# GpSimd takes the differences of the next input, and four v tiles are made later, in a two-layer attention kernel

## The chip, the cores and the metric

The kernel runs on one core of a Trainium2 chip. The metric is the device time in microseconds (us), the median of several runs. Engines are named as in the profile: PE is TensorE (PEld its weight loads), DVE is VectorE, ACT is ScalarE, POOL is GpSimd, and SP is SyncE, which here only issues DMAs.

## The reference, cut to what matters

Two attention layers run on `x` of shape (8, 512, 32, 32): 8 batches, 512 channels, 1024 positions, all float32. Layer 1, the only one that the change touches, is

```
y    = group_norm(x)                                # input of layer 1
q, k, v = w_q y, w_k y, w_v y                       # 512x512 products, 8 heads of 64
attn = softmax(w_head mixed over heads(q k^T * scale))
attn = (attn - mean) / sqrt(var + eps) * gamma + beta   # over a whole head
x    = x + w_proj (attn v) + b_proj
```

The mix over heads needs the scores of all 8 heads for the same query and key, before the exponential.

## The kernel before, in words

Layer 0 runs first, for all batches (up to about 1790 us of the profile). Layer 1 then runs batch by batch, each taking some 273 us. What follows is about layer 1.

**Order.** Nothing schedules at run time: each engine carries out its own instructions in the order in which the Python code issues them, waiting on semaphores where it depends on another engine or on a DMA. SP has one such queue for nearly all DMAs. An `Agenda` holds small jobs by slot number; `ag.at(slot, fn)` enters one, and `Attention1.step` (L1857) calls `ag.run` with fixed slots: 4p-0.5 and 4p-0.25 around the first mix of step p, 4p+0.5 and 4p+1.5 in its middle, and 4p+t at the end of quarter t.

**Steps.** A batch has nine steps, p = 0 to 8, each of four quarters t = 0 to 3. Step p makes eight score tiles for block p of the queries (`scores`, L1630), unless p = 8, and finishes the mix of block p-1 and the weighted values of blocks p-1 and p-2.

- `scores` writes a PSUM tile of 128x1024. There are three such tiles (tag `m`), taken in turn by scores, mixes, projections and v tiles. A copy (ACT L1642; in the first step every second one DVE L1640) takes it to SBUF as `raw`. Scores 0 to 3 fill one `raw` buffer and 4 to 7 the other; there are two.
- `regroup` (L1648) moves `raw` to `re` by 16 DMAs of 256 KB a step, 8 for each half, all in SP's queue. A half's buffer is free for the next step's copies when its 8 DMAs have landed.
- `mix` (L1667) multiplies `re` with the head weights into two of the PSUM tiles, and ACT takes the exponential `e` (L1680). DVE transposes it (`flip`, `et`, L1695, two buffers) and takes its statistics (`moments`, `bn`, L1709).
- `values` (L1725) multiplies `et` with `v`. Three times a batch (after blocks 1, 3 and 5) POOL's queue sends reciprocals to DRAM and reads them back spread over the partitions in two halves (`zd`, `rzb`, L1773 and L1783), and POOL multiplies a quarter of the output by them (`divide`, L1810).

**v tiles.** A batch has eight tiles of `v`. `v_pair(b, i)` makes tiles 2i and 2i+1 with four products each (L1456), and ACT and DVE copy them out of PSUM (L1462). Pairs 0 and 1 are made before the batch starts, pairs 2 and 3 (`NV` and `NV + 1`) inside it. `v_pair` reads the input `y_t[b]` and the weights `wv`, and `wv` lies in one of the two `et` buffers.

**The next input.** In steps 1 to 4, at the end of quarter 0, `piece` issues one transfer of 512 KB each of the next batch's input: `y_piece` (L1339), in SP's queue. The tile that it fills has the tag `n`, in a pool with one buffer: it is the buffer of this batch's `y`. In the last batch the pieces are weights instead (`p_piece`, L1333), with a buffer of their own.

**The ninth step.** In step 8 no scores are left, and the first four of the seven products of the next batch's k projection stand between the mixes (`k_go`, PE L1381). Some read `right_t`, four differences of blocks of the next `y`, each of 128x1024, made by `combine_right` (L1356); products 6, 7, 5 and 4 read the second, third, first and fourth difference. The buffer of `right_t` is one of the two of `raw`. Each product has a follower on ACT or DVE, such as `u = u + product` (L1396, L1398).

Of the kernel before, what the change touches and what calls it, by code (L numbers as in the profile page):

```python
# [467 lines left out]
def tile_two_attention_layers(  # L468
# [19 lines left out]
    nc = tc.nc  # L488
# [4 lines left out]
    NT = T // P  # L493
# [172 lines left out]
    def group_stages(b0, b1, psum):  # L666

        gs = GroupStats(
            gstat, psum, mvs[:, b0:b1].rearrange("p b c s -> p (b c) s"), f"1_{b0}", keep=1
        )  # L670

        def end():
            gs.root()
            at = slice(b0 * NCC, b1 * NCC)
            nc.vector.tensor_copy(gmean[:, at], gs.gm)
            nc.vector.tensor_copy(grstd[:, at], gs.r1)
            nc.vector.scalar_tensor_tensor(
                gneg[:, at], gs.gm, -1.0, gs.r1, ALU.mult, ALU.mult
            )
            nc.vector.scalar_tensor_tensor(  # L680
                ys[:, b0:b1].rearrange("p b c -> p (b c)"), gs.dm, float(T), gs.r1,
                ALU.mult, ALU.mult,
            )

        return gs.means, gs.squares, end
# [13 lines left out]
    with ExitStack() as l0:  # L699
# [177 lines left out]
        def combine_right(nm, n):  # L877

            if not tmp:
                for i in range(7):  # L880
                    tmp[i] = epool.tile([P, 2, FB], F32, tag="e", name=f"tmp_{nm}_{i}")
            b11, b12, b21, b22 = (n[:, 2 * i : 2 * i + 2, ts(j, FB)] for i in (0, 1) for j in (0, 1))
            nc.vector.tensor_sub(tmp[0], b12, b11)
            nc.vector.tensor_sub(tmp[1], b22, tmp[0])
            nc.vector.tensor_sub(tmp[2], b22, b12)
            nc.vector.tensor_sub(tmp[3], b21, tmp[1])
# [318 lines left out]
        for b in range(B):  # L1205
            more = b + 1 < B
            ag = Agenda()
# [61 lines left out]
    with ExitStack() as l1:  # L1269
# [15 lines left out]
        def m_psum(nm):  # L1285
            return ps_m.tile([P, 2, FB], F32, tag="m", name=nm)
# [4 lines left out]
        y_t, qo_t, k_t, v_t = ({0: t["1"]} for t in (n_t, q_t, k_t, v_t))  # L1291
# [12 lines left out]
        def left_piece(key, f, n):  # L1304

            if f == 0:
                left_tile(key)
            nc.sync.dma_start(
                out=w_t[key][:, f : f + n].rearrange("p f o -> p (f o)"),
                in_=left_d[key[0] + "1"][:, 2 * f * HC : 2 * (f + n) * HC],  # L1310
            )
# [23 lines left out]
        def y_piece(b, c):  # L1335

            if c == 0:
                y_t[b] = shared.tile([P, NCC, T], F32, tag="n", name=f"y_{b}")
            nc.sync.dma_start(out=y_t[b][:, c], in_=x1_d[b][ts(c, P), :])  # L1339

        def normalize1(b, c):
            normalize_to(y_t[b][:, c], b, c)
# [5 lines left out]
        def quarters(n):  # L1348
            return [[n[:, 2 * i : 2 * i + 2, ts(j, FB)] for j in range(2)] for i in range(2)]

        def combine_right(t, n, parts=range(4)):

            (b11, b12), (b21, b22) = quarters(n)
            for i in parts:
                x, y = ((b12, b11), (b22, t[:, 0]), (b22, b12), (b21, t[:, 1]))[i]
                nc.vector.tensor_sub(t[:, i], x, y)  # L1356

        class Projection:
            ORDER = (1, 6, 2, 7, 5, 3, 4)
# [55 lines left out]
        right_t = {}  # L1415

        def right_tile(b):

            right_t[b] = rawpool.tile([P, 4, 2, FB], F32, tag="raw", name=f"right_{b}")

        def left_p(b):

            t = rawpool.tile([P, H * FB], F32, tag="raw", name=f"left_p_{b}")
            load_left(("p", b), t[:, : 14 * HC])

        def right_y(b, parts=range(4)):
            combine_right(right_t[b], y_t[b], parts)

        def k_projection(b):
            t = k_t[b] = shared.tile([P, NCC, T], F32, tag="k", name=f"k1_{b}")  # L1430

            def finish(i, j, x, y):
                dst = t[:, 2 * i : 2 * i + 2, ts(j, FB)]
                if y is None:
                    nc.scalar.copy(dst, x)
                else:
                    nc.vector.tensor_add(dst, x, y)

            return Projection(f"pk1_{b}", ("k", b), y_t[b], right_t[b], finish)
# [3 lines left out]
        def k_leave():  # L1443
            for fn in due:
                fn()
            due.clear()

        def v_pair(b, i, ms=range(2)):

            if i == 0:  # L1450
                v_t[b] = shared.tile([P, NT, C], F32, tag="v", name=f"v1_{b}")
            ps = m_psum(f"pv1_{b}_{i}_{ms[0]}")
            w = w_t["v", b]
            for m in ms:
                for c in range(NCC):
                    nc.tensor.matmul(  # L1456
                        ps[:, m], y_t[b][:, c, ts(2 * i + m, P)], w[:, c],
                        start=(c == 0), stop=(c == NCC - 1),
                    )
            for m in ms:  # L1460
                copy = nc.vector.tensor_copy if m else nc.scalar.copy
                copy(v_t[b][:, 2 * i + m], ps[:, m])  # L1462
# [478 lines left out]
        NV = NT // 4  # L1941
        for b in range(B):
            more = b + 1 < B
            a = Attention1(b)
            ag = Agenda()
            ag.at(1, lambda: v_pair(b, NV))
            ag.at(3, lambda: v_pair(b, NV + 1, [0]))
            ag.at(3.75, lambda: v_pair(b, NV + 1, [1]))
            if b == 0:
                stages = group_stages(B - 1, B, small_psum1)  # L1950
                for i in range(3):
                    ag.at(i, stages[i])
                ag.at(3, v_sums)
            if more:
                a.pieces += [lambda c=c: y_piece(b + 1, c) for c in range(NCC)]
                a.pieces += [lambda f=f: left_piece(("k", b + 1), f, 2) for f in (0, 4)]
                ag.at(4 * NT, lambda: left_piece(("k", b + 1), 2, 2))
                ag.at(4 * NT, lambda: left_piece(("k", b + 1), 6, 1))
                for c in range(NCC):
                    ag.at(20 + c, lambda c=c: normalize1(b + 1, c))  # L1960

                def k_go(*ms):
                    if not kp:
                        kp.append(k_projection(b + 1))
                    for m in ms:
                        kp[0].products(m)
                        due.append(lambda m=m: kp[0].leave(m))

                kp = []
                ag.at(4 * NT - 0.5, lambda: right_tile(b + 1))  # L1970
                ag.at(4 * NT - 0.5, lambda: k_go(1))
                ag.at(4 * NT, lambda: right_y(b + 1, [0, 1]))
                ag.at(4 * NT + 0.5, lambda: k_go(2))
                ag.at(4 * NT + 1, lambda: right_y(b + 1, [2, 3]))
                ag.at(4 * NT + 1, lambda: left_p(b))
                ag.at(4 * NT + 1.5, lambda: k_go(6))
                ag.at(4 * NT + 2.5, lambda: k_go(7))
            else:
                a.pieces += [lambda c=c: p_piece(c) for c in range(NCC)]
            for p in range(NT + 1):  # L1980
                for t in range(4):
                    a.step(p, t, ag)
            ag.flush()
            k_leave()
            last = NT - 1
            a.sums(NCH - 1)
            if not more:
                a.values(last, 0, 2, 3)
                a.leave(last, 0)
                a.values(last, 1, 0, 1, 2, 3)  # L1990
                a.leave(last, 1)
                a.totals(NCH - 1)
                a.broadcast(1)
                a.instance()
                out1_last(a)
                continue
            k_go(5)
            a.values(last, 0, 2, 3)
            a.leave(last, 0)
            load_wv(b + 1)  # L2000
            a.values(last, 1, 0, 1, 2, 3)
            a.leave(last, 1)
            a.totals(NCH - 1)
            a.broadcast(1)
            a.instance()
            k_leave()
            k_go(4, 3)
            k_leave()
            a.instance_end()
            v_pair(b + 1, 0)  # L2010
            a.divide(NCH - 1)
            for g in range(H):
                a.affine(g)
            right_o = re_t[:, 4:8]
            combine_right(right_o, out_view(b))
            op = out1(b, right_o)
            load_left(("q", b + 1))
            v_pair(b + 1, 1)
            a.check()
            op.run()  # L2020
            q_projection(b + 1).run()
# [70 lines left out]
```

## Time and profile before

| | us |
|---|---|
| median of 3 runs | 3967.3 (3964.85 to 3968.17) |
| the profiled execution, its own time | 3964.89 |
| its span, from first to last instruction | 3963.1 |
| PE busy | 3874.9 (98% of the span) |
| DVE busy | 2769.6 (70%) |
| ACT busy | 1971.4 (50%) |
| POOL busy | 141.2 (4%) |
| mean granted clock of PE | 0.996 |

The times of single instructions come from the profiled execution. A row of the timeline gives the start in the span, the duration, engine, line, operation, the tile written and those read, the shape, and in brackets how long the engine stood idle just before and what ended that. Rows of SP (marked SPq) are the issue of a DMA, not its transfer. A matmul's end is modelled, so a PE that is busy is not always a PE at its peak.

### The profile page before, as it was taken

Reading aid. Unit: us, or ns where it says so; the run is one execution under the profiler, and the core shown is the slowest. Engines: PE = TensorE matmul, PEld = TensorE weight load, DVE = VectorE, ACT = ScalarE, POOL = GpSimd, SP = SyncE. Lnnn points to the kernel's source line nnn. Section 1 sums busy time; section 2 is a strip of 40 time slices with the busy share of each in tenths; the row PEclk is TensorE's granted clock in tenths of the full one; section 3 lists DMA queues with packets and bytes.
Section 4 is the critical chain, followed back from the end, with each engine's and each line's share of the span. In section 5 each row is a group of like instructions: output and inputs, shape, how many; then the busy total and the mean of one; then the engine's idle time right before and its main releaser. Section 6 shows DMA issues by size and latency. Waiting matters only on the chain.

```text
span 3963.1 us, 95453 instructions
## 1 busy us (share of the span) xinstructions
PE 3874.9 (98%) x41868; PEld 1823.7 (46%) x41868; DVE 2769.6 (70%) x3741; ACT 1971.4 (50%) x2431; POOL 141.2 (4%) x182
## 2 busy tenths in 40 slices
PE   8999999999999999999999999999999999999997
PEld 4353535344353535344544545545545445445454
DVE  4747475665757474856967958859768679588596
ACT  1726354453627172624716718538347267175284
POOL 0000000000000000000100100001001001000010
PEclk9999999999999999999999999999999999999998
DMA  3313131121121121216938839749568478397494
GB/s 121 123 48 117 47 118 46 55 73 65 55 72 68 61 76 48 89 49 173 230 114 208 211 104 237 198 119 236 158 158 220 134 192 226 98 229 191 124 226 124
DMA packets 249593, 519.09 MB, mean 131 GB/s; under 512 B 51024, under 2 KB 58192, under 8 KB 242512
## 3 DMA queue, kind: packets, MB, share of 16 engines
q1 hardware_dynamic: 241984, 500.08, 44.2%
q0 software_dynamic: 7184, 12.81, 1.5%
q8 instruction: 331, 5.42, 0.6%
q14 instruction: 94, 0.77, 0.1%
HBM read 197.16 MB, written 46.92 MB: 62 GB/s over the span
## 4 chain that ended last, share of the span: by engine, by line
PE 90%; DVE 5%; DMA 3%; ACT 1%; issue 1%; SPq 0%; ACTq 0%; DVEq 0%
PE s L1086 11%; PE a L1112 11%; PE a L1725 11%; PE s L1630 10%; PE m L1667 6%; PE pk_p L904 6%; PE pq_p L904 5%; PE pv L1456 5%; PE pv_p L904 5%; PE pp_p L904 5%; PE pq L1381 4%; PE pp L1381 4%; PE pk L1381 3%; DMA re<-raw 3%; DVE et L1695 1%; DVE bn L1709 1%
## 5 line engine op out<-in xcount | busy, mean ns | idle before, releaser
L1695 DVE STREAM_TRANSPOSE et<-e 128x2048 f32<-128x2048 f32 x256 | 589.5, 2303 | 100.0 <-ACT e L1680 99.0
L1725 PEld LDWEIGHTS a<-et,v 128*64 128x64 f32 x16384 | 510.8, 139 | 296.4 <-issue 273.4
L1709 DVE BATCH_NORM_STATS2 bn<-e 128x6 f32<-128x512 f32 x1024 | 635.1, 681 | 0.0
L1091 ACT ACTIVATE e<-s 128x1024 f32<-128x1024 f32 x512 | 497.2, 1026 | 233.8 <-PE s L1086 233.4
L1642 ACT COPY raw<-s 128x1024 f32<-128x1024 f32 x480 | 470.2, 1018 | 211.6 <-PE s L1630 179.0
L1680 ACT ACTIVATE e<-m 128x1024 f32<-128x1024 f32 x512 | 496.3, 1021 | 156.1 <-issue 56.3
L1725 PE MATMUL a<-et,v 128*64 128x64 f32 x16384 | 558.9, 225 | 11.2 <-DVE et L1695 7.8
L1099 DVE TENSOR_TENSOR zacc<-zacc,e 128x1024 f32<-128x1024 f32 x384 | 468.7, 1221 | 87.8 <-ACT e L1091 65.5
L1630 PE MATMUL s<-k,q 64*64 64x512 f32 x4096 | 515.2, 607 | 5.8 <-DVE q L1496 3.2
L1086 PE MATMUL s<-q,k 64*64 64x512 f32 x4096 | 490.1, 593 | 2.3 <-ACT e L1091 2.3
L1112 PE MATMUL a<-e,v 64*64 64x512 f32 x4096 | 484.1, 589 | 0.0
L1667 PE MATMUL m<-re,wmix 32*32 32x512 f32 x8192 | 311.0, 602 | 19.5 <-DMA re<-raw 16.5
L1112 PEld LDWEIGHTS a<-e,v 64*64 64x64 f32 x4096 | 156.7, 133 | 282.8 <-issue 282.2
L1086 PEld LDWEIGHTS s<-q,k 64*64 64x64 f32 x4096 | 147.9, 133 | 275.2 <-issue 240.5
L1630 PEld LDWEIGHTS s<-k,q 64*64 64x64 f32 x4096 | 127.8, 132 | 220.8 <-issue 87.1
L1456 PE MATMUL pv<-wv,y 128*128 128x512 f32 x480 | 214.3, 599 | 0.0
L1773 POOL DMA_DIRECT2D zd<-rz x96 | 52.5, 552 | 3508.2 <-DVE rz L1767 3506.0
L1741 ACT COPY q<-a 64x256 f32<-64x256 f32 x256 | 94.0, 367 | 148.3 <-PE a L1725 146.2
L1456 PEld LDWEIGHTS pv<-wv,y 128*128 128x128 f32 x480 | 88.6, 190 | 119.8 <-issue 106.5
L1667 PEld LDWEIGHTS m<-re,wmix 32*32 32x32 f32 x8192 | 68.8, 103 | 162.4 <-ACT raw L1642 69.3
L1462 DVE COPY v<-pv 128x512 f32<-128x512 f32 x30 | 20.7, 689 | 159.5 <-PE pv L1456 80.9
L1097 DVE TENSOR_TENSOR zacc<-e,e 128x1024 f32<-128x1024 f32 x64 | 78.3, 1223 | 55.9 <-ACT e L1091 55.9
(317 smaller groups left out, 3866.4 us busy)
## 6 DMA issues: line engine op xcount, KB each, us to landing
re<-raw SPq DMA_DIRECT2D x1024, 256.0 KB
left_q<-left_q SPq DMA_DIRECT2D x17, 1792.0 KB
left_p<-left_p SPq DMA_DIRECT2D x17, 1792.0 KB
left_k<-left_k SPq DMA_DIRECT2D x10, 1792.0 KB
x<-in_x_dram SPq DMA_DIRECT2D x32, 512.0 KB
rzb<-zd SPq DMA_DIRECT2D x128, 128.0 KB
x<-x SPq DMA_DIRECT2D x64, 256.0 KB
y<-x SPq DMA_DIRECT2D x32, 512.0 KB
```

What stands on the lines that cost most here:

```text
L904: nc.tensor.matmul(out, st, mv, start=start, stop=(k == 1), skip_group_check=True)
L1086: nc.tensor.matmul(ps[c * D : c * D + D, m], k[r, hp, k0 : k0 + D], q[r, hp, ts(f, FB)], start=True, stop=True,)
L1091: nc.scalar.activation(e[i], ps, AF.Exp, scale=S0 * S0)
L1112: nc.tensor.matmul(acc[g][a][m * D : m * D + D], v[rows, kc, ts(2 * hp + m, D)], e[i][rows, m], start=(kc == 0), stop=(kc == NG - 1),)
L1456: nc.tensor.matmul(ps[:, m], y_t[b][:, c, ts(2 * i + m, P)], w[:, c], start=(c == 0), stop=(c == NCC - 1),)
L1630: nc.tensor.matmul(ps[c * D : c * D + D, m], qo_t[b][r, p, hp, ts(c, D)], k_t[b][r, hp, ts(kh, FB)], start=True, stop=True,)
L1642: nc.scalar.copy(dst, ps)
L1667: nc.tensor.matmul(ps[a // 2][c * 32 : c * 32 + 32, a % 2].rearrange("p (r h k) -> p h r k", r=2, h=2), wmix[rows].rearrange("p g i -> p ( ...
L1680: nc.scalar.activation(e[:, :, 2 * h : 2 * h + 2].rearrange("p r a k -> p a r k"), ps[h].rearrange("p a (r k) -> p a r k", r=2), AF.Exp,)
L1695: nc.vector.transpose(self.et[p, u].rearrange("p kb (r st a) g q -> p st kb r (a g q)", r=2, st=2)[:, st], self.e[p, s].rearrange("p r a ( ...
L1709: nc.vector.bn_stats(self.bn[n][:, p % 2, s, a], e[:, :, a].rearrange("p r k -> p k r"))
L1725: nc.tensor.matmul(acc[two * D : two * D + D, s].rearrange("p (x q) -> p x q", q=4), v_t[b][:, kb, ts(g, D)], et[:, kb, :, g], start=(kb = ...
```

## The change

Two things are changed. All four differences of the next `y` are made by GpSimd instead of VectorE, and all four are issued together ahead of the first mix of the ninth step (slot 4 NT - 0.5) instead of two after it and two a quarter later. And the v tiles are moved: pair `NV` from the end of the first step's quarter 1 to the end of its quarter 3, behind the eighth score; the first tile of pair `NV + 1` from there to behind the first mix of the second step; the second one from there to the second step's quarter 2, behind its sixth score and ahead of its third mix.

```diff
-        def combine_right(t, n, parts=range(4)):
+        def combine_right(t, n, parts=range(4), engine=nc.vector):
 
             (b11, b12), (b21, b22) = quarters(n)
             for i in parts:
                 x, y = ((b12, b11), (b22, t[:, 0]), (b22, b12), (b21, t[:, 1]))[i]
-                nc.vector.tensor_sub(t[:, i], x, y)
+                engine.tensor_sub(t[:, i], x, y)
...
         def right_y(b, parts=range(4)):
-            combine_right(right_t[b], y_t[b], parts)
+            combine_right(right_t[b], y_t[b], parts, nc.gpsimd)
...
             ag = Agenda()
-            ag.at(1, lambda: v_pair(b, NV))
-            ag.at(3, lambda: v_pair(b, NV + 1, [0]))
-            ag.at(3.75, lambda: v_pair(b, NV + 1, [1]))
+            ag.at(3, lambda: v_pair(b, NV))
+            ag.at(3.75, lambda: v_pair(b, NV + 1, [0]))
+            ag.at(5.5, lambda: v_pair(b, NV + 1, [1]))
...
                 ag.at(4 * NT - 0.5, lambda: right_tile(b + 1))
                 ag.at(4 * NT - 0.5, lambda: k_go(1))
-                ag.at(4 * NT, lambda: right_y(b + 1, [0, 1]))
+                ag.at(4 * NT - 0.5, lambda: right_y(b + 1))
                 ag.at(4 * NT + 0.5, lambda: k_go(2))
-                ag.at(4 * NT + 1, lambda: right_y(b + 1, [2, 3]))
```

## The prediction

> **What bounds the kernel now.** I read the busy table first: PE is busy 98% of the span, so only two things can gain or cost: a stretch in which PE waits, and one in which it will begin to. The waits of PE over layer 1 say which exist:
>
> ```profile
> PE m L1667 <- DMA re<-raw: 16.5, 15, 3.8
> PE pk L1381 <- DVE re L1398: 8.2, 7, 1.2
> PE pk L1381 <- DVE right L1356: 2.6, 7, 0.4
> ```
>
> The columns are us in total, times, longest. Rows two and three occur once per change of batch (7): the ninth step. Its timeline, DVE and PE, at the first change:
>
> ```profile
> 1995.24 1.21 DVE L1356 TENSOR_TENSOR right<-y 128x1024 f32<-128x1024 f32 x1
> 1996.36 1.22 DVE L1356 TENSOR_TENSOR right<-y,right 128x1024 f32<-128x1024 f32 x1
> 1997.50 1.21 DVE L1396 TENSOR_TENSOR re<-re,pk 128x1024 f32<-128x1024 f32 x1
> ...
> 1996.59 3.67 PE L1381 MATMUL pk<-right,left_k 128*128 128x512 f32 x8 [0.36 <-DVE right L1356]
> 2004.52 3.70 PE L1381 MATMUL pk<-right,left_k 128*128 128x512 f32 x8 [1.17 <-DVE re L1398]
> ```
>
> Two differences stand on DVE ahead of L1396, the transpose and L1398; PE waits for the first of them, then for L1398.
>
> For the v tiles I read the second step of batch 1, with SP and ACT beside PE:
>
> ```profile
> 2106.52 3.70 PE L1456 MATMUL pv<-wv,y 128*128 128x512 f32 x8
> 2110.25 0.34 SPq L1339 DMA_DIRECT2D y<-x  x1
> 2112.34 15.13 SPq L1648 DMA_DIRECT2D re<-raw  x16
> 2123.97 2.85 ACT L1642 COPY raw<-s 128x1024 f32<-128x1024 f32 x3 [0.76 <-DMA re<-raw]
> 2124.83 2.08 PE L1725 MATMUL a<-et,v 128*64 128x64 f32 x64
> ...
> 2126.84 1.14 PE L1667 MATMUL m<-re,wmix 32*32 32x512 f32 x32
> ```
>
> The last v tile ends at 2106.52 + 3.70 = 2110.22, and the transfer of the next `y` is issued 0.03 us later: it overwrites the buffer that this product reads. SP's waits over layer 1 have it by name, once per batch but the last:
>
> ```profile
> SPq L1339 <- PE pv L1456: 29.4, 7, 6.7
> ```
>
> The second step's regroups stand behind it in SP's queue. Today that costs nothing: they need the score copy that ends at 2112.32 anyway. But ACT's next three copies, of the third step's scores, wait until the first eight have landed (2123.97), and the mix at 2126.84 needs two of those copies, since it needs two of three PSUM tiles. The second ends about 2125.9: PE has 0.9 us in hand there, no more. By stretches, the DMA engines are full (columns: us, busy time of PE, PEld, DVE, ACT, POOL, PE's clock, DMA share, GB/s):
>
> ```profile
> 2110.00:2114.00 4.00, 3.87 (x53) 0.87 (x56) 3.74 (x4) 2.55 (x3) 0.00 (x0) 1.00 0.56 163
> 2114.00:2122.00 8.00, 7.70 (x152) 3.04 (x144) 8.00 (x9) 6.81 (x8) 0.00 (x0) 1.00 1.02 249
> 2124.00:2140.00 16.00, 16.00 (x368) 9.06 (x363) 15.00 (x18) 13.35 (x17) 0.00 (x0) 1.00 1.03 253
> ```
>
> **What the Trainium skill says.** "DMA: Bandwidth & Descriptors", Issuing engines are not separate DMA queues: all DMAs run on the same 16 engines and interleave. The trace agrees: a share of 1.02 at 249 GB/s is full, so transfers that start late end late. "SBUF — State Buffer", SBUF: two separate sides: a VectorE operation with two SBUF inputs and a GpSimd one that reads SBUF exclude each other; the later blocks. The trace agrees: the difference at 2801.43 took 1.74 us instead of 1.21, beside GpSimd's `divide` that ended at 2802.09. "GPSIMD Engine Reference", Elementwise: a two-input operation is 1.96 times slower than on VectorE. Here `divide` takes 2.356 us on POOL and 1.215 on DVE, 1.94 times. "TensorE: Matmul & The Clock Gate", What's actually happening: an idle window of about 3.4 us, free-running, halves PE's clock. The trace shows the half clock for 3.41 us after a wait of 1.98 us (1938.04), and none after 1.7 us (2170.17).
>
> **The change, part by part.**
>
> *Differences.* Four DVE operations of 1.21 us leave the ninth step of 7 batches: 4.8 us of DVE each. L1396 moves from 1997.5 to the end of `bn` at 1995.3; the transpose follows at 1996.5 (its input is ready at 1996.35), `bn` at 1998.7, L1398 at 2001.2 to 2002.4. PE, ready for that product at 2004.52 - 1.17 - 0.36 = 2003.0, no longer waits. Up to the next scores (2083.7) PE has no further wait, so all 0.36 + 1.17 = 1.53 us reach the end: 8.2 + 2.6 = **10.8 us** over 7 batches. After L1398 the last transpose (ready 2003.1, done 2005.4) is next, ahead of the values at 2006.6.
>
> POOL takes the four at 2.36 us: 9.4 us. No row shows when their buffer comes free; DVE started at 1982.20 with no wait, so not later. Started only then, the second difference is done at 1986.9, the third at 1989.3, all at 1991.6; their products start at 1989.44 and 1996.2. Covered in the worst case. On POOL's queue the second broadcast (1972.62) and `divide` (1979.37) fall behind them, to about 1992 and, 6.75 us later, 1998 to 2001. The quarter divided is read from 2031.4 on, so nothing waits. Beside the differences DVE runs transposes and statistics of one input. Cost: 0, at worst all of the 10.8 is lost if POOL is late.
>
> *v tiles, first step.* The sum of PE's products is the same. Scores 4 to 7 come 7.1 us earlier, so their regroups follow the first eight without a pause; no mix there waits for DMA today, so no gain. The wait for `et` after the seventh score of step 2 (0.30 us, 8 times, 2.4 us) goes, since the transposes no longer stand behind the last v tile's copy. But that copy (0.69 us) now stands behind a transpose and `bn` on DVE, and a score needs its PSUM tile: about as much. I take 0 (bounds -2.4 and +3). The last read of `wv` frees the second `et` buffer at about 2114.6; the transpose into it starts at 2120.1 today, so there are 5 us of cover.
>
> *v tiles, second step.* In the changed kernel's order the `y` transfer still stands between the first step's regroups and the second's, and it waits for the last v tile. In the order of PE that tile moves behind a score (2110.15 to 2111.17), a mix (to 2112.37) and two scores (to 2114.56): 4.4 us. So `y` goes at about 2114.65 and the first regroup 0.4 later, at 2115.05 instead of 2112.34, though its data is there at 2109. `y` and eight regroups are 0.52 + 8 x 0.26 = 2.62 MB, 10.5 us at 250 GB/s. Today 13.7 us pass from the issue of `y` to ACT's copy: 3.2 of start and of a pause (share 0.56 from 2110 to 2114). The pause shrinks, as the regroups now follow in 0.4 us instead of 2.1: I take 13.1 (12.4 to 13.7). ACT's copy then starts at 2127.75, 3.8 late, and two copies end at 2129.7. PE, done with the values at 2126.8, waits **2.9 us** (2.2 to 3.5), 7 times. The waits of ACT in the other six batches look the same (DMA 0.5 us in batch 3, 1.3 in batch 5), so there is no more slack there. Everything behind moves with it, the DMAs too; the next regroups wait for their scores. In the last batch no `y` is moved, and its weights have their own buffer: 0.
>
> An idle time of 2.9 us lies between the 1.98 that halved the clock and the 3.4 window: up to 3.41 x 0.5 = 1.7 us more each, at least 0. PE has other waits there; I take 0.9.
>
> *Sum.* 7 x (2.9 + 0.9) - 10.8 = 26.6 - 10.8 = **+15.8 us**. On the profiled execution's 3964.9 that is 3980.7; the median of the runs is 2.4 above it: **3983 us**. This measurement can tell some 0.2%, 8 us, from no change.
>
> **The rivals.**
>
> *The transfer is hidden anyway: faster.* If regroups behind `y` land in time, because SP's queue or the DMA engines have more slack than ACT's wait shows, only the ninth step remains, with the 2.4 us: -10.8 to -13.2, about 3955. For it: DMA pauses at 2122 (share 0.85), and step 2 has no PE wait for DMA. Against: in batches 1, 3 and 5 ACT already waits for exactly this landing, with 0.9 us between it and PE.
>
> *The two cancel: within 0.2%.* If the stall is 1 to 2 us, as the pause vanishes, the clock stays whole and later waits of the mixes (16.5 us in all, most in the fifth and seventh step) shrink by what PE is late: 7 x 1.5 = 10.5 against 10.8, about 3967, 3960 to 3975.
>
> *GpSimd is late too: slower still.* If its differences wait for broadcasts or for DVE, so that product 6 (1989.44) waits, the 10.8 go and more: 3994. Against: 2.5 us of cover from a start at 1982.2, and POOL is free from 1973.1 on.
>
> That the change does not do what it says is excluded: the built order has four subtractions per batch on POOL between the two broadcasts, and the v tiles where the diff puts them.
>
> **How the numbers follow.** Forecast with its neighbour of a late GpSimd 0.65 (3975 to 3996), cancelling 0.19, hidden 0.16. Slower by over 0.2% begins at 3975: 0.65; within: 0.19; faster: 0.16. The likeliest case's own range is 3975 to 3996. The range for 8 in 10 reaches down into the hidden case, 3957 to 3996.
>
> **What would show it.** Right: the wait of PE `pk` for DVE gone; a new wait of the mix, 2 to 3.5 us in step 3 of seven batches, ended by ACT's `raw` copy, which itself waits some 4 us for `re<-raw`; SP's wait of L1339 for PE `pv` longer by some 8 us a batch (4.4 from the move, 4 from an SP that is done earlier); the half clock behind it. Wrong: regroups of step 2 that start before the last v tile ends, or no wait at that mix. Then the total would be 3955, and if PE `pk` waits for POOL, the first part failed.

## The result and the profile after

The changed kernel takes 3983.6 us (median of 6 runs, 3980.15 to 3993.46), the kernel before on the same chip 3965.8 (6 runs, 3961.72 to 3968.17). The ratio is 1.0054, with an interval of 1.0044 to 1.0063: slower by half a per cent. The profiled execution took 3981.72 us, its span 3979.9, which is 16.8 more than before.

The busy table of the changed kernel (first part of its page: us, share of the span, instructions) shows that PE has no more work than before (3874.9 then). What is new is waiting. DVE has given up 30 us, POOL has taken 66:

```profile
PE 3873.1 (97%) x41868; PEld 1825.8 (46%) x41868; DVE 2740.0 (69%) x3713; ACT 1970.5 (50%) x2431; POOL 207.3 (5%) x210
```

PE's waits over layer 1 (us in total, times, longest):

```profile
PE m L1667 <- DMA re<-raw: 28.8, 17, 3.6
PE m L1667 <- ACT raw L1642: 20.5, 14, 4.6
PE s L1630 <- DVE v L1462: 3.6, 8, 0.5
PE pk L1381 <- DVE re L1396: 2.1, 6, 0.4
```

The rows of `pk` on L1398 (8.2 us) and on `right` (2.6) are gone; a small one on L1396 has come. The waits of the mixes have grown from 16.5 + 2.1 to 28.8 + 20.5; the 2.1 stand in this row of the kernel before:

```profile
PE m L1667 <- ACT raw L1642: 2.1, 3, 0.7
```

SP's wait for the last v tile is three times what it was (29.4 before):

```profile
SPq L1339 <- PE pv L1456: 98.8, 7, 17.8
```

One of the seven places, the second step of batch 1 and the mix after it, in the timeline of SP, PE and ACT:

```profile
2113.12 3.70 PE L1456 MATMUL pv<-wv,y 128*128 128x512 f32 x8
...
2116.86 0.34 SPq L1339 DMA_DIRECT2D y<-x  x1
2117.30 14.17 SPq L1648 DMA_DIRECT2D re<-raw  x16
...
2126.37 2.08 PE L1725 MATMUL a<-et,v 128*64 128x64 f32 x64
2129.82 2.84 ACT L1642 COPY raw<-s 128x1024 f32<-128x1024 f32 x3 [5.08 <-DMA re<-raw]
2131.69 2.12 PE L1667 MATMUL m<-re,wmix 32*32 32x512 f32 x32 [3.23 <-DMA re<-raw]
```

The last v tile ends at 2116.82, `y` goes 0.04 us later, then the sixteen regroups, which ACT's copies and the mix wait for. The same mix waits 3.52, 3.23, 4.56, 3.04, 2.56, 3.28 and 2.92 us in the first seven batches, and not at all in the last one, in which no `y` is moved.

The other place, the ninth step, at the same change of batch as in the prediction:

```profile
1980.95 2.41 POOL L1356 TENSOR_TENSOR right<-y 128x1024 f32<-128x1024 f32 x1 [6.41 <-DMA re<-raw]
...
1988.14 2.39 POOL L1356 TENSOR_TENSOR right<-y,right 128x1024 f32<-128x1024 f32 x1
...
1998.01 1.19 DVE L1396 TENSOR_TENSOR re<-re,pk 128x1024 f32<-128x1024 f32 x1
1999.35 3.67 PE L1381 MATMUL pk<-right,left_k 128*128 128x512 f32 x8 [0.35 <-DVE re L1396]
2006.03 3.70 PE L1381 MATMUL pk<-right,left_k 128*128 128x512 f32 x8
```

POOL has all four differences done at 1990.5, before the first product that reads one starts (1992.21). The product that waited 1.17 us for L1398 starts at 2006.03 without a wait. From the start of the first `pk` record to that of the last the ninth step takes 41.75 us instead of 43.00.

Where the 16.8 us of the span come from, by intervals between the same instructions of the two traces, summed over the batches:

| stretch | predicted | measured |
|---|---|---|
| ninth step, first to last `pk` | -10.8 | -9.7 |
| first score to the mix in step 2's quarter 3 | 0 | +4.5 |
| from there to the first mix of step 3 (6.92 us before, 9.55 to 11.55 after) | +20.3 | +23.5 |
| from there to the next mix (3.17 us before): half clock | +6.3 | +6.1 |
| all else | 0 | -7.6 |

### The profile page after: what moved, and what is told of

It reads as the page before. It is cut to its first block, busy times and chain, and to the rows that moved or that the text cites. A ratio compares the mean times of both kernels' runs of the same rounds, so it can differ in the third digit from the quotient of the medians.

```text
span 3979.9 us, 95460 instructions
## 1 busy us (share of the span) xinstructions
PE 3873.1 (97%) x41868; PEld 1825.8 (46%) x41868; DVE 2740.0 (69%) x3713; ACT 1970.5 (50%) x2431; POOL 207.3 (5%) x210
## 5 line engine op out<-in xcount | busy, mean ns | idle before, releaser
L1667 PE MATMUL m<-re,wmix 32*32 32x512 f32 x8192 | 306.4, 605 | 49.7 <-DMA re<-raw 28.8
L904 PE MATMUL pv_p<-left_v,tmp 128*128 128x256 f32 x512 | 113.1, 379 | 0.0
```

The source lines that it names most:

```text
L1667: nc.tensor.matmul(ps[a // 2][c * 32 : c * 32 + 32, a % 2].rearrange("p (r h k) -> p h r k", r=2, h=2), wmix[rows].rearrange("p g i -> p ( ...
```

## The experiments

Every ratio is against the kernel before, run on the same chip; times are medians.

**The differences alone**, on the kernel before.

```diff
-                nc.vector.tensor_sub(t[:, i], x, y)
+                engine.tensor_sub(t[:, i], x, y)
...
-            combine_right(right_t[b], y_t[b], parts)
+            combine_right(right_t[b], y_t[b], parts, nc.gpsimd)
...
-                ag.at(4 * NT, lambda: right_y(b + 1, [0, 1]))
+                ag.at(4 * NT - 0.5, lambda: right_y(b + 1))
...
-                ag.at(4 * NT + 1, lambda: right_y(b + 1, [2, 3]))
```

> The kernel before with only the differences moved to GpSimd and ahead of the ninth step's first mix; the v tiles stay. Theory (the two parts are independent; the ninth step gives 1.25 us in each of 7 batches, as the trace of the changed kernel shows, where 0.36 of the forecast 1.53 came back as a wait for L1396): 8.8 us less than before, about 3957. Rival A (GpSimd is part of what made the changed kernel slower, through its port or its DMA queue): no gain, 3966 or more.

Measured: 3951.1 us against 3961.7, ratio 0.9964 (0.9950 to 0.9978). The ninth step takes 41.75 us in all seven batches and the third step's first mix never waits. This half of the change is worth its 10 us, and a kernel with it alone beats both.

**The v tiles alone**, on the kernel before.

```diff
-            ag.at(1, lambda: v_pair(b, NV))
-            ag.at(3, lambda: v_pair(b, NV + 1, [0]))
-            ag.at(3.75, lambda: v_pair(b, NV + 1, [1]))
+            ag.at(3, lambda: v_pair(b, NV))
+            ag.at(3.75, lambda: v_pair(b, NV + 1, [0]))
+            ag.at(5.5, lambda: v_pair(b, NV + 1, [1]))
```

> The kernel before with only the v tiles moved. Theory (the input's transfer, held by the last v tile, holds the second step's regroups in SP's queue; 3.3 us and part of a half-clock window in each of 7 batches): about 26 us more than before, 3992, with the mix of the third step waiting 2.5 to 4.6 us in seven batches. Rival A (GpSimd is the cause): no change, 3966.

Measured: 3998.6 us, ratio 1.0081 (1.0064 to 1.0098). The stall is in the same seven places, 21.0 us in all. All of the loss lies in this half, and it is above the loss of the whole change by about what the differences bring: 1.0081 x 0.9964 = 1.0045, against 1.0054. The 37 us are more than the expected 26. In this trace the half clock behind the stall costs 8.4 us, and the forecast had left out two stretches: the one up to the mix in step 2's quarter 3 is 5.9 us longer, and the ninth step 2.7.

**The last v tile back in its old place**, in the changed kernel: the `y` transfer no longer waits so long, all else stays.

```diff
-            ag.at(5.5, lambda: v_pair(b, NV + 1, [1]))
+            ag.at(3.75, lambda: v_pair(b, NV + 1, [1]))
```

> The changed kernel with the last v tile moved back ahead of the second step's first quarter end (slot 3.75), so that only the first pair and the tile before it stand later than in the kernel before. The input's buffer is then free where it was before. Theory: no stall in the third step, about 3957. Rival B (the order of the v tiles costs, whichever they are): most of the cost stays, 3975 to 3984.

Measured: 3957.8 us, ratio 0.9992 (0.9985 to 0.9998). The interval to the third step's first mix is back at 6.92 us in every batch, so the stall is gone. The kernel is still slower than the one with the differences alone (0.9964); 8.1 us of that lie in the stretch up to the mix in step 2's quarter 3, where the other three v tiles still stand later.

**The `y` transfer behind the first eight regroups of the second step**, in the changed kernel: the last v tile stays late, but nothing stands behind the transfer that waits for it.

```diff
-                a.pieces += [lambda c=c: y_piece(b + 1, c) for c in range(NCC)]
+                ag.at(6, lambda: y_piece(b + 1, 0))
+                a.pieces += [lambda: None]
+                a.pieces += [lambda c=c: y_piece(b + 1, c) for c in range(1, NCC)]
```

> The changed kernel, with the first 512 KB transfer of the next input issued behind the second step's first eight regroups instead of ahead of them; v tiles and differences as changed. Theory (SP's queue is what holds): the third step's mix does not wait, 24 us less than the changed kernel, about 3958. Rival B (the new order of the v tiles itself costs, by PSUM tiles and copies): the stall stays, 3984.

Measured: 3954.7 us, ratio 0.9977 (0.9969 to 0.9986). 6.92 us again, in all batches, and SP's row for L1339 on `pv` is gone. So neither the late tile by itself nor its 3.7 us of PE make the stall; it takes the transfer that waits for it at the head of SP's queue.

**The hold alone**, on the kernel before, v tiles and differences in their old places: a tiny product that reads `y`, issued where the changed kernel has its last v tile. Its result is not used.

```diff
+            def read_y(b):
+                ps = m_psum(f"hold_{b}")
+                nc.tensor.matmul(
+                    ps[:, 0, :8], y_t[b][:, 0, :P], ones[:, :8], start=True, stop=True
+                )
...
+                ag.at(5.5, lambda: read_y(b))
```

> The kernel before, v tiles and differences as they were, with one added product of 8 columns (its result is not used) that reads the current input at slot 5.5, where the changed kernel's last v tile reads it. So the input's transfer is held as in the changed kernel, and nothing else is moved. Theory (the hold in SP's queue is the whole cost): the third step's mix waits 3 to 3.5 us in seven batches, 23 us and some half-clock windows, 25 to 35 us more than before. Rival B (the new places of the v tiles cost): at most 2 us more, for eight small products.

Measured: 3993.2 us, ratio 1.0069 (1.0056 to 1.0083), 29 us slower. The timeline of batch 1:

```profile
2115.47 0.39 PE L1951 MATMUL hold<-ones,y 128*128 128x8 f32 x2
2115.89 0.34 SPq L1339 DMA_DIRECT2D y<-x  x1
...
2116.34 13.82 SPq L1648 DMA_DIRECT2D re<-raw  x16
...
2128.64 2.84 ACT L1642 COPY raw<-s 128x1024 f32<-128x1024 f32 x3 [4.53 <-DMA re<-raw]
2130.40 1.35 PE L1667 MATMUL m<-re,wmix 32*32 32x512 f32 x32 [2.58 <-DMA re<-raw]
```

0.39 us of PE, seven times, costs 29 us, since it is the last reader of the buffer that `y` overwrites. This kernel shows the stall (21.5 us by intervals) and the half clock behind it (10.0 us more to the next mix) with no v tile moved.

**Is it the late start, or `y`'s bytes ahead of the regroups?** In the changed kernel the first transfer was cut in two: 64 KB in the old place, so that SP is held just as long, and 448 KB behind the first eight regroups.

```diff
+        def y_part(b, lo, hi):
...
+            nc.sync.dma_start(out=y_t[b][:, 0, lo:hi], in_=x1_d[b][:P, lo:hi])
...
-                a.pieces += [lambda c=c: y_piece(b + 1, c) for c in range(NCC)]
+                a.pieces += [lambda: y_part(b + 1, 0, P)]
+                ag.at(6, lambda: y_part(b + 1, P, T))
+                a.pieces += [lambda c=c: y_piece(b + 1, c) for c in range(1, NCC)]
```

> The changed kernel with the first 512 KB of the next input cut in two: 64 KB go where the whole went, and are held by the last v tile in the same way; 448 KB go behind the second step's first eight regroups. It tells the two halves of the delay apart. If the 2.1 us that 512 KB take on the DMA engines ahead of the regroups are part of it: the wait of the third step's mix falls from 3.4 us to about 1.5, 13 us less than the changed kernel in seven batches, still about 5 us above the kernel before. If only the late start in SP's queue counts: the wait stays above 3 us, and the time at the changed kernel's.

Measured: 4002.3 us, ratio 1.0100 (1.0084 to 1.0115): neither outcome, slower than the changed kernel itself. The stall is 4.9 us a batch. Its timeline (line numbers are 5 higher in this kernel, the small transfer and the rest are both L1344):

```profile
2117.82 0.34 SPq L1344 DMA_DIRECT2D y<-x  x1
2118.57 6.89 SPq L1653 DMA_DIRECT2D re<-raw  x8
...
2125.50 1.06 SPq L1344 DMA_DIRECT2D y<-x  x1
2126.66 7.22 SPq L1653 DMA_DIRECT2D re<-raw  x8
...
2130.00 2.84 ACT L1647 COPY raw<-s 128x1024 f32<-128x1024 f32 x3 [4.27 <-DMA y<-x]
...
2133.92 1.48 PE L1672 MATMUL m<-re,wmix 32*32 32x512 f32 x32 [4.49 <-DMA re<-raw]
```

ACT's first copy starts when the eighth regroup has landed (2129.9), though its row names `y`. Two copies end at about 2131.9, yet the mix starts 2 us later, on a landing. It needs the first two DMAs of *both* halves. By the DMA records of the trace the tenth regroup lands at 2133.8, 3.9 us after the eighth; in the changed kernel the two land at 2129.6 and 2131.6. The 448 KB between the halves are the 1.9 us of difference. So there is a second way to the same mix, and the run had moved the bytes onto it.

**The same, with the 448 KB behind all sixteen regroups** (slot 7 for slot 6 in the diff above).

> The changed kernel, with 64 KB of the first y transfer in the old place (it waits for the last v tile as before, so it holds SP's queue just as long) and the other 448 KB behind all sixteen regroups of the second step instead of between its halves. If the hold makes the stall by starting the regroups late, the first mix of the third step still waits, but with 448 KB less ahead of the regroups, 1.8 us at 250 GB/s, so for some 1.5 us in each of seven batches instead of 3.4: about 3970 us. If y's bytes ahead of the regroups make it and the hold nothing, there is no wait and the time is that with the whole transfer moved, about 3955. If the small transfer itself is what costs (the run with the rest between the halves was slower than the changed kernel), the stall stays near 5 us and the time near 4000.

Measured: 3984.7 us, ratio 1.0062 (1.0048 to 1.0075). The stall is 3.1 us a batch (2.9 to 3.3): the late start makes it. I had expected the missing 448 KB to save 1.8 us; they save 0.3. By stretches (us, busy PE, PEld, DVE, ACT, POOL, PE's clock, DMA share, GB/s), this kernel in the first two us after its transfer was issued at 2113.96, and in the next two:

```profile
2114.00:2116.00 2.00, 1.55 (x40) 0.30 (x31) 1.40 (x3) 0.80 (x1) 0.00 (x0) 1.00 0.16 48
2116.00:2118.00 2.00, 2.00 (x44) 1.22 (x40) 0.83 (x1) 2.00 (x3) 0.00 (x0) 1.00 0.96 246
```

and the changed kernel after its own at 2116.86:

```profile
2117.00:2119.00 2.00, 1.55 (x40) 0.21 (x8) 1.29 (x3) 0.90 (x1) 0.00 (x0) 1.00 0.53 115
2119.00:2121.00 2.00, 2.00 (x46) 1.22 (x40) 0.93 (x1) 1.94 (x3) 0.00 (x0) 1.00 0.98 312
```

In its first four us the changed kernel moves 854 KB (230 and 624), the other 588 KB: a transfer of `y` fills the start-up of the first regroups, and with it the engines also move more per us. From the issue of `y` to ACT's copy it is 12.96 us in the changed kernel and 12.68 here.

**The `y` transfer and the half that is good.** The differences alone, with the `y` transfer behind the first eight regroups, as in the run above that took the stall away.

```diff
-                a.pieces += [lambda c=c: y_piece(b + 1, c) for c in range(NCC)]
+                ag.at(6, lambda: y_piece(b + 1, 0))
+                a.pieces += [lambda: None]
+                a.pieces += [lambda c=c: y_piece(b + 1, c) for c in range(1, NCC)]
```

> The kernel before with the differences on GpSimd (v tiles as before) and the first transfer of the next input behind the second step's first eight regroups. Theory: in the old order of the v tiles the transfer holds nothing, since the regroups wait for a score copy 2.1 us later anyway; so the same as with the differences alone, 10 us less than before, or 1 to 2 us better, as the DMA pause ahead of the regroups holds no transfer any more. If the third step had hidden waits on the landing of the regroups, more: up to 15 us less than before.

Measured: 3964.3 us, ratio 1.0004 (0.9996 to 1.0013). The gain of the differences is lost again; the third step's first mix is 0.9 to 2.2 us late in each of the seven batches. The timeline of batch 1:

```profile
2119.21 0.60 SPq L1339 DMA_DIRECT2D y<-x  x1
...
2121.20 6.21 SPq L1648 DMA_DIRECT2D re<-raw  x8
...
2128.67 1.15 PE L1667 MATMUL m<-re,wmix 32*32 32x512 f32 x32 [1.65 <-DMA re<-raw]
```

Here the first eight regroups end at 2119.2 in SP's queue and the next eight begin at 2121.2, so `y` runs while the engines are still full (share 1.07 from 2119 to 2121). In the changed kernel with the same edit the v tiles lie otherwise: `y` goes at 2115.5 and the second half at 2118.9, the share is 0.73 from 2115 to 2117 and 0.65 from 2119 to 2121, and `y` fits into the pause. That the length of the pause makes the difference is read from these two traces; no run changes it alone.

**The same, with `y` behind all sixteen** (slot 7 for slot 6).

> The kernel before with the differences alone on GpSimd and the first y transfer behind all sixteen regroups of the second step, not between the halves. If the 10 us that were lost with y between the halves came from its bytes ahead of the second half's regroups, they come back: about 3951 us, ratio 0.9964, no wait of the third step's first mix. If a later y collides with whatever regroups follow it, the wait only moves, to the third or fourth step, and the time stays near 3962.

Measured: 3951.6 us, ratio 0.9973 (0.9965 to 0.9980), and 6.92 us in every batch. The 10 us are back, so what took them were `y`'s bytes between the halves. The Trainium skill, "DMA: Bandwidth & Descriptors", Issuing engines are not separate DMA queues, has transfers interleave on the same 16 engines; these two runs agree, with 0.9 to 2.2 us a batch for 512 KB put ahead of what a mix needs.

**The changed kernel with `y` behind all sixteen.**

> The changed kernel, whole, with the first y transfer behind all sixteen regroups of the second step. No hold is left in SP's queue ahead of the regroups, so no stall in the third step: 3951 to 3957 us, as with y behind the first eight (3954.7 there). If the later y takes the DMA engines from the third step's regroups, the mixes of the fourth step wait for them instead, and it is slower than that, 3960 or more.

Measured: 3961.0 us, ratio 0.9994 (0.9986 to 1.0002). No stall in the third step, but not the expected 3951 to 3957 either. PE's waits of the mixes for regroups and for ACT's copies sum to 31.1 us, against 26.1 with `y` behind the first eight. But the fourth step's first mix, which the other outcome names, waits 1.0 us in all eight batches together, against 0.7 there. Most of the difference lies at the first mixes of the fifth and seventh step: 8.0 and 7.3 us, against 5.9 and 5.1 there, and 6.1 and 7.7 in the kernel before. So the time is that of the other outcome, but its cause is not seen, and why this kernel is slower stays open.

## Why the prediction was right, step by step

**The stall.** The chain was as written: last v tile, `y` behind it in SP's queue, regroups behind `y`, ACT's copies behind the regroups, the mix. The hold alone makes it, and either end of the chain taken away unmakes it. It was 3.4 us a batch instead of 2.9. In batch 1, the time from the issue of `y` to ACT's copy was 12.96 us (13.1 estimated). PE's work in the same time was 11.6 us (2116.86 to 2128.46), not 12.2, and this term was mis-sized: the 12.2 were taken from the trace of before, in which a mix after the v tile (2114.56) lasted 1.94 us, while the same mix lasts 1.14 in the changed kernel (2116.75). 0.8 us of what was counted as work were waiting inside a row: its matmuls start in four groups from 2114.56 to 2115.91, in the changed kernel within 0.6 us. A wait for the v tile's copy of 0.45 us, where 0.30 for `et` stood, takes some of that back.

**What ends it.** I had named ACT's copy alone. Four of the seven waits are ended by the landing of a regroup. The tenth lands at 2131.6 in batch 1, ACT's second copy ends at 2131.7: both ways are equally long, and the run with the small transfer showed the second one by making it longer. For the size this made no difference; for what one would mend, it does.

**Half clock.** 6.3 us were predicted and 6.1 measured, but in other portions: 1.5 to 2.7 us in three batches and next to nothing in four, not 0.9 each. That the sums agree is luck. Two of the seven places in the changed kernel, by stretches:

```profile
2131.00:2137.80 6.80, 6.11 (x88) 2.75 (x104) 1.85 (x1) 4.33 (x7) 0.00 (x0) 0.50 0.96 253
2689.00:2692.40 3.40, 3.40 (x88) 1.59 (x72) 0.40 (x1) 3.36 (x6) 0.00 (x0) 1.00 1.07 283
```

After 3.23 us of waiting the clock was 0.50 for 6.8 us, after 3.04 us it stayed at 1.00. Three of the seven places got the half clock.

**The ninth step.** L1396, the transpose and L1398 moved forward as worked out, and the 1.17 us are gone. Of the 1.53 us only 1.25 came (the 9.7 us of the table hold another 1.0, of two batches whose ninth step took longer in the kernel before), since the 0.36 wait for `right` was followed by one of 0.35 for L1396. The reason is in the built programs. The PSUM tile of a product is one of three, chosen as the program is built. In the kernel before, products 6 and 7 lie in different tiles, and 7 need not wait for L1396, which reads 6. In the changed kernel, and in that with the differences alone, both lie in the same tile in all seven batches. "Taken in turn" was too simple for it, and the cost is 0.3 us, 7 times. POOL was earlier than the prediction's worst case: its first difference starts 11.3 us before the first product that reads one (1980.95 and 1992.21), where the worst case had 7.2 (1982.20 and 1989.44). The broadcast and `divide` behind it cost nothing that shows in PE's waits.

**The first step.** 0 was predicted (-2.4 to +3), +4.5 measured. The wait for `et` went and the one for the v tile's copy came (3.6 us, 8 times), as said. Two batches make the rest: in batches 3 and 4 the first mix of step 2 waited 2.32 and 2.39 us for regroups, with the half clock after the second one. In most other batches it waits 0.9 to 1.2 us for ACT's copy, which takes back the time that the earlier scores and the shorter mix in quarter 3 had brought. So the "no gain" was right, but there was a loss that the bounds did not reach. The runs without the stall bear it out in direction: with the `y` transfer behind the first eight regroups the changed kernel is at 0.9977, with the last v tile back at 0.9992, and the differences alone are at 0.9964; the same stretch is 3.7 and 8.1 us longer in the first two.

**All else.** The -7.6 us were not in the sum. 4.5 of them lie around the seventh step's first mix. PE's waits there are only 1.0 us shorter (6.7 us in eight batches against 7.7), but the kernel before has two windows at half clock there (3.41 us each, from 1939.02 and 3034.69, behind waits of 1.98 and 1.21 us) where the changed kernel has none. This need not come from the change: in the traces of all ten experiments, with a stall and without, this stretch is 3.2 to 6.8 us shorter than in the profiled execution of the kernel before. So the shrinking of later waits that the rival of cancelling named is not shown. The other 3.1 us I cannot place; single batches of the same code differ by more than that between runs. So the closeness of the total (+16.8 against +15.8) is in part luck: the terms of the sum came out 8.6 us too low together, and these 7.6, which were not in it, took most of that back.

**The rivals.** Hidden (3955) fell with the stall; it is where the kernel goes once the transfer is out of the way (3954.7). Cancelling (3960 to 3975) needed a stall of 1 to 2 us. A late GpSimd (3994) did not occur.

## What to carry to other kernels

A DMA that overwrites a buffer makes the last reader of that buffer part of its queue: whoever moves the last reader moves everything that stands behind the DMA, and a product of 0.39 us can cost 29. So for each edit ask which transfer is released by it and what is queued behind that transfer, and put such a transfer behind those that feed the critical engine, in a place where the DMA engines pause. And a change of two halves is worth taking apart: one was good for -10.6 us, the other for +37, and the good one alone beat both kernels (3951.1 us).

## What the runs showed of the hardware that was not expected

- **Near 3 us the half clock came in some places, near 5 in all.** The Trainium skill, "TensorE: Matmul & The Clock Gate", What's actually happening, has a free-running window of about 3.4 us. Over the six us around the end of each stall, the mean clock was under 1.00 in 3 of 7 places of the changed kernel (stalls of 2.6 to 4.6 us), in 6 of 7 behind the hold alone (2.4 to 4.0 us), in 3 of 7 with 448 KB behind all regroups (2.9 to 3.3 us), and in 7 of 7 with them between the halves (4.6 to 5.2 us). One half-clock window costs 1.3 to 1.8 us at the next mix. The traces agree with a window that runs freely: in the changed kernel the half clock starts at 1806.70, 2130.97, 2410.86, 2936.51 and 3513.36, the later four 95, 177, 331 and 500 times 3.413 us after the first. They differ from the page in one point: the window need not be idle throughout. What fits is how busy PE was in a window of this grid, and so where the stall falls on it. Of the 28 places above, 17 have a window in which PE was busy for at most 40%, and the half clock followed in all 17; in the other 11 the emptiest window was busy for 41 to 53%, and it followed in two. The rows below are a window of batch 1 (a stall of 3.23 us) with PE busy for 0.90 us, which the half clock followed, and one of batch 3 (3.04 us) with 1.42 us, which it did not.
- **A transfer ahead can be nearly free.** In batch 1, 448 KB ahead of the regroups cost 0.3 us, while they filled the start-up, and 1.9 us between two halves, when the engines were full.
- **The place decides, not the size.** `y` behind the first eight regroups took the stall away in one kernel (ratio 0.9977 instead of 1.0054) and lost the gain in the other (1.0004 instead of 0.9964); the second half followed after 3.4 us of pause in the first and 2.0 in the second. Behind all sixteen it was the other way round: worse in the first (0.9994), without loss in the second (0.9973).

The two windows of the first point:

```profile
2127.56:2130.97 3.41, 0.90 (x32) 0.76 (x26) 1.92 (x4) 1.15 (x2) 0.00 (x0) 1.00 1.07 275
2683.91:2687.32 3.41, 1.42 (x50) 1.28 (x44) 2.44 (x5) 0.79 (x1) 0.00 (x0) 1.00 1.05 273
```
